# Smaller array tiles in window attention, other slots in two scans, a rewritten last MLP, and x loaded in quarters

## The chip, the cores and the metric

The kernel runs on one core of one Trainium2 chip. A core has five engines with their own instruction streams: TensorE (matrix multiply; the profile shows its matmuls as PE and its weight loads as PEld), VectorE (DVE), ScalarE (ACT), GpSimd (POOL) and SyncE (SP), which here issues all DMAs. They meet through semaphores only. The metric is the device time of one execution in microseconds (us); a lower time is better. All data are float32 unless said otherwise.

## The reference, cut to what matters

Four images of 256 channels and 64x64 pixels go one after the other through four layers. Layers one and two are the same attention block with other weights, layer three is a Mamba block with inner width 512 and 16 states, layer four ("grouped") runs a Mamba of inner width 128 on each of four groups of 64 channels, followed by an MLP. The core of each:

```python
# attention (layers 1 and 2): after a group norm, two gated 1x1 paths and a scan over rows give y
q, k, v = split(to_windows(y) @ qkv_w.T + qkv_b)       # 64 windows of 64 pixels
idx = top_k(mean(q) @ mean(k).T, 4)                     # each window picks 4 windows
attn = softmax((q * C**-0.5) @ k[idx].T)                # 8 heads of 32 channels, 64 queries, 256 keys
out = from_windows(attn @ v[idx]) + depthwise3x3(v)     # "lepe"
x = x + out @ wo.T + wo_b
# Mamba (layers 3 and 4)
u = silu(causal_conv4(in_proj(norm(x))))
dt, B, C = split(x_proj(u));  delta = softplus(dt_proj(dt))
h[t] = exp(delta[t] * A) * h[t-1] + delta[t] * u[t] * B[t]
y[t] = sum_n C[t, n] * h[t, :, n] + D * u[t];   m = y * silu(z) @ out_proj
# layer 4 then, per group
m = gelu(layernorm(m) @ fc1 + b1) @ fc2 + b2 + skip * xn
out = x + silu(batchnorm(outc @ m))
```

## The kernel before

Channels lie on the 128 partitions, in two halves; x of one image (128 x 8192) stays in on-chip memory from its load until the last layer has added its result and stored it. `net_kernel` loops over the four images: it loads x with two DMAs (L1934), then calls `attention_layers`, `mamba_layer` and `grouped_mamba_layer`. The tile pools use a manual schedule: each engine runs its instructions in the order in which the Python code emits them, and waits only where a tile is not ready or a buffer not free.

**Attention.** Each of the two layers has a scan phase over 8 strips of 8 image columns (`scan_phase`), a routing step, and a window phase (`window_phase`) over 32 pairs of windows. One turn `i` of the pair loop emits, in this order: the gathers of pair i+2 (DMA), `scores(i + 1)`, the softmax parts `smallest`, `exps` and `normalise` of pair i+1 interleaved with `turn` and `turned` of pair i (the transposes of the probabilities on TensorE and the copies out of PSUM), one projection of 1x1 kind (`queries` or `project`), and `values(i)`. `own_rows(i - 1)` adds the attention output to the image of the depthwise convolution. GpSimd normalises the probabilities and does 36 of the depthwise taps (`taps`, spread over the first 27 turns). In the first attention layer steps of the next layer's group norm (`gn`) are placed on turns, in the second the statistics of x for the next norm (`stats`); both put instructions on VectorE, ScalarE, GpSimd and TensorE by the dictionaries `mids` and `ends`.

The query tile `qbuf` holds each 64-row block twice, with two heads side by side and zeros where the other head stands, so that one matmul of 64 rows by 128 columns gives the scores of two heads for 64 queries. The zeros are written once per image by 16 memsets (L105). A pair needs 16 score matmuls and 16 value matmuls; in the records each float32 matmul is two passes, each with its weight load. A value matmul takes 128 rows by 64 columns, and yields for two heads also the products of one head's probabilities with the other head's values; `own_rows` takes the rows that belong to each head, in four additions of 32 rows.

**The scans.** `scan_blocks` runs both Mamba layers. A block is 128 inner channels by 1024 pixels, a slot is one of its 16 states. Per slot VectorE multiplies `du` with the broadcast B (`pb`, L914) and scans (L920), GpSimd multiplies with the broadcast C (`hc`, L926), ScalarE computes the decay (L856; `dap` where it lies in PSUM), and TensorE broadcasts B from a table split into bfloat16 parts (`spread`, L844) and sums up y through transposes (`turn`, L872). Three states of a block are treated "apart": their B comes by DMA and GpSimd does the multiplication (L830). All else of the layer, for the next block or the one before, is placed by hand on slots: `put(block, slots, steps)` appends steps to a slot's list `bg`, which the loop emits after that slot's scan. The steps that matter here are `x_proj` (projections, then two copies on ScalarE and two subtractions on GpSimd that split the table: `xs`), `delta` (softplus: a matmul, then Abs, Exp and Ln on ScalarE, then an addition on VectorE, per half; last the product `du` on GpSimd), `silu` (needs another table set on ScalarE, and back), `mlp` (seven steps for each half of 512 pixels), `norm`, `out_conv` and `out`. In the grouped layer a chunk of 1024 pixels has four blocks, two pairs of an `even` and an `odd` block.

**The end of an image.** After the last block of the grouped layer the code emits the rest of the MLP of the pair before (`late`), then the last pair's MLP one half after the other with all table changes, then four output convolutions, their Silu, four additions on GpSimd and the stores. Then the next image's x is loaded.

Of the kernel before, what the change touches and what calls it, by code (L numbers as in the profile page):

```python
# [24 lines left out]
NH = 4  # L25
# [20 lines left out]
class Net:  # L46
# [33 lines left out]
    def attention_layers(self, x, w_drams, v_drams):  # L80
        tc, nc = self.tc, self.nc
        with ExitStack() as ctx:
# [17 lines left out]
                [big.tile([P, 2, NW, 2, 64], F32, name=f"q{i}{m}") for m in range(2)]  # L100
                for i in range(2)
            ]
            for t in qbuf[0] + qbuf[1]:
                for r in range(0, P, 32):
                    nc.gpsimd.memset(t[r : r + 32, :, :, 1 - r // 32 % 2, :], 0.0)  # L105
# [151 lines left out]
            def queries(lay, s, m, psum):  # L257
# [4 lines left out]
                def evict():  # L262
                    for h in range(NH):
                        rows = slice(h * 32, h * 32 + 32)
                        b, h2 = divmod(h, 2)
                        nc.scalar.activation(
                            q[rows, b, :, h2, :].rearrange("p w (j i) -> p w j i", i=8),
                            ps[rows].rearrange("p (j w i) -> p w j i", j=8, i=8),
                            AF.Identity, bias=lay["neg_bq"][rows, m : m + 1], scale=-SCALE,
                        )  # L270
# [163 lines left out]
            def window_phase(lay, work, psum, idx, nxt):  # L434
# [31 lines left out]
                sc = {}  # L466
# [3 lines left out]
                def scores(i):  # L470
                    sj, a = divmod(i, 4)
                    for w in range(2 if i < n_pair else 0):
                        sc[w] = psum.tile([P, 2, 4, P], F32, tag="sc", name="sc", bufs=2)
                        t = kv[i, w]
                        for cq in range(4):
                            m, b = divmod(cq, 2)
                            for r in range(2):
                                rows = slice(r * 64, r * 64 + 64)
                                k0 = b * P + m * 64
                                nc.tensor.matmul(  # L480
                                    sc[w][:, r, cq, :],
                                    qbuf[sj % 2][m][rows, b, 2 * a + w].rearrange("p h t -> p (h t)"),
                                    t[rows, :, k0 : k0 + 64], start=True, stop=True,
                                )

                mn = {}

                def smallest(i, w):
                    if i < n_pair:
                        mn[w] = self.small.tile([P, 4], F32, tag="mn", name="mn", bufs=4)  # L490
                        nc.vector.tensor_reduce(  # L491
                            mn[w], sc[w].rearrange("p r c n -> p c r n"), AX.XY, ALU.min
                        )

                def exps(i, w, part=range(4)):
                    if i < n_pair:
                        if 0 in part:
                            sm[i, w] = self.small.tile([P, 4], F32, tag="sm", name="sm", bufs=4)
                            pr[i, w] = work.tile([P, 4, 2, 2, 64], F32, tag="pr", name="pr", bufs=2)
                        t = pr[i, w]  # L500
                        for cq in part:
                            nc.scalar.activation(  # L502
                                t[:, cq].rearrange("p j r t -> p r j t"),
                                sc[w][:, :, cq, :].rearrange("p r (j t) -> p r j t", j=2),
                                AF.Exp, bias=mn[w][:, cq : cq + 1], scale=-1.0,
                                accum_out=sm[i, w][:, cq : cq + 1],
                            )

                def normalise(i, w):
                    if i < n_pair:  # L510
                        t, s = pr[i, w], sm.pop((i, w))
                        nc.vector.reciprocal(s, s)  # L512
                        t = t.rearrange("p c j r t -> p c (j r t)")
# [7 lines left out]
                def turn(i, w):  # L521
                    pt[w] = [
                        psum.tile([P, 4, P], F32, tag="pt", name="pt_ps", bufs=2) for j in range(2)
                    ]
                    t = pr.pop((i, w))
                    for j in range(2):
                        for cq in range(4):
                            nc.tensor.transpose(  # L528
                                pt[w][j][:, cq, :], t[:, cq, j].rearrange("p r t -> p (r t)"),
                                self.ident,  # L530
                            )
                    pts[w] = [
# [4 lines left out]
                def turned(w, j):  # L537
                    if j == 0:
                        nc.vector.tensor_copy(pts[w][0], pt[w][0])
                    else:  # L540
                        nc.scalar.activation(pts[w][1], pt[w][1], AF.Copy)  # L541

                def values(i, w):
                    if w == 0:
                        ov[i] = psum.tile([P, 2, 2, 8, 2, 8], F32, tag="ov", name="ov_ps", bufs=1)
                    t = kv.pop((i, w))
                    for m in range(2):
                        for j in range(2):
                            for b in range(2):
                                cq = 2 * m + b  # L550
                                c0 = C + cq * 64
                                nc.tensor.matmul(  # L552
                                    ov[i][b * 64 : b * 64 + 64, m, :, :, w, :],
                                    t[:, j, c0 : c0 + 64], pts[w][j][:, cq, :],
                                    start=(j == 0), stop=(j == 1),
                                )


                def own_rows(i):
                    if i >= 0:  # L560
                        sj, a = divmod(i, 4)
                        for r in range(4):
                            rows = slice(r * 32, r * 32 + 32)
                            out = vimg[rows, :, 8 * sj : 8 * sj + 8, 1 + a * 16 : 17 + a * 16]
                            nc.vector.tensor_tensor(  # L565
                                out, ov[i][rows, :, r % 2].rearrange("p m j w i -> p m j (w i)"),
                                out, ALU.add,
                            )
                        del ov[i]
# [20 lines left out]
                for w in range(2):  # L590
                    smallest(0, w)
                    exps(0, w)
                    normalise(0, w)
# [26 lines left out]
                for i in range(n_pair):  # L620
# [35 lines left out]
                    values(i, 0)  # L656
                    values(i, 1)
# [457 lines left out]
    def mamba_layer(self, x, bridge, pe_dram, w_in, w_cw, w_x, w_dt, w_out, v_dram):  # L1115
        tc, nc = self.tc, self.nc
        ND = 4
        with ExitStack() as ctx:
# [228 lines left out]
            for k in range(n_chunk):  # L1347
# [27 lines left out]
                if more:  # L1375
# [25 lines left out]
                    put(3, (7, 8, 8, 9, 9, 10, 11, 12), xs)  # L1401
                    put(3, (9, 10, 10, 11, 12), delta(k + 1, 0))
# [88 lines left out]
    def grouped_mamba_layer(self, x, bridge, begun, ws_dram, outc_dram, v_dram, out_b):  # L1491
        tc, nc = self.tc, self.nc
        w_in, w_cw, w_x, w_dt, w_out, w_f1, w_f2 = ws_dram
        with ExitStack() as ctx:
# [212 lines left out]
            def out_conv(k, s, m):  # L1707
                def step():
# [6 lines left out]
                    if s == 0 and m == 0:  # L1715
                        chunks[k]["yo"] = work.tile([P, 4, NT], F32, tag="hid", name="yo", bufs=1)
                    nc.scalar.activation(
                        yo(k, s, m), ps, AF.Identity, bias=bnb[:, m : m + 1], scale=bns[:, m : m + 1]
# [13 lines left out]
            def out(k, s, m):  # L1732
                def step():
                    t0 = k * NC + s
                    xs = x[:, m * T + t0 : m * T + t0 + NT]
                    nc.gpsimd.tensor_tensor(yo(k, s, m), xs, yo(k, s, m), ALU.add)
# [115 lines left out]
            for i, (k, c) in enumerate(pairs):  # L1852
# [12 lines left out]
                if more:  # L1865
                    h0, h1 = (self.later(lambda k=k, s=s: norm(k + 1, s), 5) for s in range(2))
                    put(even, (0,), (lambda k=k: begin(k + 1),))
                    put(even, (0, 1, 4, 5, 6), h0)
                    put(even, (14, 15), h1)
                    put(odd, (1, 2, 3), h1[2:])  # L1870
                put(even, (4, 5, 6, 7, 8, 9), x_proj(k, 2 * c + 1))
                if i:
                    m0, m1 = mlp(*pairs[i - 1], 0), mlp(*pairs[i - 1], 1)
                    put(even, (5, 6, 7, 10, 11, 12, 13), m0)
                    put(even, (6, 7, 8), m1)
# [3 lines left out]
                    else:  # L1879
# [150 lines left out]
```

## Time and profile before

| | us |
|---|---|
| median of 3 runs (12438.44 to 12444.25) | 12441.65 |
| the profiled execution, its own time | 12439.35 |
| its span, first to last instruction | 12437.6 |
| mean granted TensorE clock (share of full speed) | 0.922 |
| period from image to image (x loads to x loads) | about 3109 |
| window phases of the second image | 3340 to 3625 and 3820 to 4125 |
| scan of the Mamba layer, same image | 4180 to 5150 |
| scan of the grouped layer, same image | 5220 to 6140 |

The profile is one execution, taken by the hardware profiler. In a group's line stand the source line, the engine, the operation, the tile written and those read, the shape, the count, the busy time with the mean duration of one, and the idle time before it with what ended most of it. The chain of waits, followed back from the last instruction, holds only some 18% of the span here, all in the last image, so stages are read one by one instead. Some of the rows that carry the work of the window phase:

```profile
L514 POOL TENSOR_TENSOR pr<-pr,sm 128x1024 f32<-128x1024 f32 x512 | 967.9, 1897 | 560.0 <-DVE sm L512 380.6
L552 PE MATMUL ov_ps<-pts,kv 128*64 128x128 f32 x8192 | 583.6, 289 | 91.6 <-DVE vimg L565 75.6
L480 PE MATMUL sc<-kv,q 64*128 64x128 f32 x8192 | 573.0, 288 | 81.7 <-DMA kv<-kv_dram 68.0
L565 DVE TENSOR_TENSOR vimg<-ov_ps,vimg 32x256 f32<-32x256 f32 x1024 | 428.1, 418 | 12.1 <-PE ov_ps L552 1.6
L266 ACT ACTIVATE q<-conv_ps,neg_bq 32x512 f32<-32x512 f32 x512 | 346.4, 677 | 25.4 <-PE conv_ps L208 19.0
```

In a matmul's row "64*128" is the part of the array it uses, rows by columns. Matmuls overlap, so a mean duration of 289 ns says less than the distance between starts.

### The profile page before, as it was taken

The numbers are of one execution on the slowest core, as the hardware profiler recorded it, in microseconds if no ns is written. First come the engines' busy times: TensorE is split into PE (matmuls) and PEld (weight loads), VectorE is DVE, ScalarE is ACT, GpSimd is POOL, SyncE is SP. The second block draws the span as 40 slices with busy tenths as digits, with TensorE's granted clock in tenths as the row PEclk, the third lists the DMA queues.
The fourth block names the chain that finished last, engine by engine and source line by source line (L and its number), as shares of the span: only waits on it lengthen the run. The fifth ranks groups of instructions, "written<-read, shape, count | busy, mean of one in ns | idle before, by whom it ended". The sixth has DMA issues, their size and how long they took to land. (4 is left out here: it accounts for less than half of the span.)

```text
span 12437.6 us, 159552 instructions
## 1 busy us (share of the span) xinstructions
PE 10255.9 (82%) x54592; PEld 6015.9 (48%) x54592; DVE 10216.3 (82%) x9130; ACT 7245.9 (58%) x13300; POOL 9018.9 (73%) x4634
## 2 busy tenths in 40 slices
PE   8987887787898788777789878877878987887777
PEld 4664544443466454444346645444434664544443
DVE  6777898897677799889767779988976777998897
ACT  4565554776466555477645655547754565554775
POOL 4666886887466688688746668868874666886887
PEclk9999998999899999899889999989988999998998
DMA  3343554454334455454433434545543343554454
GB/s 96 108 128 131 168 169 147 167 169 142 97 108 127 132 169 170 146 168 167 144 95 109 127 130 172 169 146 167 169 142 95 109 127 130 172 170 146 167 170 140
DMA packets 680299, 1773.54 MB, mean 143 GB/s; under 512 B 89120, under 2 KB 195120, under 8 KB 678464
## 3 DMA queue, kind: packets, MB, share of 16 engines
q1 hardware_dynamic: 679488, 1763.34, 43.7%
q8 instruction: 435, 7.13, 0.2%
q14 instruction: 376, 3.08, 0.1%
HBM read 1601.51 MB, written 94.37 MB: 136 GB/s over the span
## 5 line engine op out<-in xcount | busy, mean ns | idle before, releaser
L926 POOL TENSOR_TENSOR hc<-h,cb 128x1024 f32<-128x1024 f32 x2056 | 4814.1, 2350 | 988.2 <-DVE h L920 425.6
L920 DVE TENSOR_TENSOR_SCAN h<-da,m_state,pb 128x1024 f32<-128x1024 f32 x1248 | 2919.9, 2340 | 161.7 <-DVE pb L914 2.8
L872 PE MATMUL y<-ident,hc 128*128 128x128 f32 x16384 | 2371.0, 293 | 346.7 <-POOL hc L926 259.0
L872 PEld LDWEIGHTS y<-ident,hc 128*128 128x128 f32 x16384 | 2091.8, 152 | 1009.7 <-POOL hc L926 439.0
L914 DVE TENSOR_TENSOR pb<-du,pb 128x1024 f32<-128x1024 f32 x1672 | 2024.8, 1211 | 92.5 <-PE pb L844 89.3
L856 ACT ACTIVATE da<-delta,m_v 128x1024 f32<-128x1024 f32 x1672 | 1898.8, 1141 | 220.8 <-DVE h L920 204.0
L844 PE MATMUL pb<-m_parts,pick 128*128 128x512 bf16 x3312 | 1099.8, 417 | 872.2 <-DVE h L920 821.8
L502 ACT ACTIVATE pr<-sc,mn 128x256 f32<-128x256 f32 x2048 | 956.6, 478 | 770.8 <-PE pt_ps L528 551.2
L514 POOL TENSOR_TENSOR pr<-pr,sm 128x1024 f32<-128x1024 f32 x512 | 967.9, 1897 | 560.0 <-DVE sm L512 380.6
L844 PEld LDWEIGHTS <-pick 128*128 128x128 bf16 x3312 | 255.2, 101 | 1883.1 <-DVE h L920 1160.3
L920 DVE TENSOR_TENSOR_SCAN h<-da,pb 128x1024 f32<-128x1024 f32 x424 | 969.6, 2287 | 55.6 <-DVE pb L914 1.4
L830 POOL TENSOR_TENSOR bb<-du,bb 128x1024 f32<-128x1024 f32 x376 | 888.8, 2364 | 65.2 <-DMA bb<-m_cd 60.5
L491 DVE TENSOR_REDUCE mn<-sc 128x4 f32<-128x1024 f32 x512 | 609.6, 1219 | 244.9 <-PE sc L480 242.8
L920 DVE TENSOR_TENSOR_SCAN h<-dap,m_state,bb 128x1024 f32<-128x1024 f32 x288 | 672.0, 2333 | 76.2 <-ACT dap L856 63.4
L528 PE MATMUL pt_ps<-ident,pr 128*128 128x128 f32 x4096 | 571.6, 283 | 145.7 <-ACT pts L541 64.3
L208 PE MATMUL conv_ps<-att_y,att_wb 128*128 128x512 f32 x1536 | 688.8, 593 | 0.0
L856 ACT ACTIVATE dap<-delta,m_v 128x1024 f32<-128x1024 f32 x376 | 419.6, 1116 | 422.3 <-DVE h L920 298.2
L552 PE MATMUL ov_ps<-pts,kv 128*64 128x128 f32 x8192 | 583.6, 289 | 91.6 <-DVE vimg L565 75.6
L480 PE MATMUL sc<-kv,q 64*128 64x128 f32 x8192 | 573.0, 288 | 81.7 <-DMA kv<-kv_dram 68.0
L528 PEld LDWEIGHTS pt_ps<-ident,pr 128*128 128x128 f32 x4096 | 465.8, 144 | 315.4 <-issue 151.4
L480 PEld LDWEIGHTS sc<-kv,q 64*128 64x128 f32 x8192 | 515.8, 196 | 124.3 <-issue 56.1
L552 PEld LDWEIGHTS ov_ps<-pts,kv 128*64 128x64 f32 x8192 | 456.4, 141 | 217.2 <-DVE vimg L565 131.9
(270 smaller groups left out, 18063.0 us busy)
## 6 DMA issues: line engine op xcount, KB each, us to landing
cb<-m_cd SPq DMA_DIRECT2D x2048, 512.0 KB
kv<-kv_dram SPq DMA_DIRECT2D x2048, 128.0 KB
bb<-m_cd SPq DMA_DIRECT2D x376, 512.0 KB
q<-q SPq DMA_DIRECT2D x256, 256.0 KB
kv_dram<-kst SPq DMA_DIRECT2D x128, 256.0 KB
kv_dram<-vn SPq DMA_DIRECT2D x128, 256.0 KB
x<-in_x_dram SPq DMA_DIRECT2D x8, 2048.0 KB
m_pe<-in_pe_dram SPq DMA_DIRECT2D x32, 512.0 KB
```

The lines of the kernel that those rows point to most:

```text
L480: nc.tensor.matmul(sc[w][:, r, cq, :], qbuf[sj % 2][m][rows, b, 2 * a + w].rearrange("p h t -> p (h t)"), t[rows, :, k0 : k0 + 64], start= ...
L502: nc.scalar.activation(t[:, cq].rearrange("p j r t -> p r j t"), sc[w][:, :, cq, :].rearrange("p r (j t) -> p r j t", j=2), AF.Exp, bias=m ...
L514: nc.gpsimd.tensor_tensor(t, t, s.rearrange("p (a o) -> p a o", o=1).to_broadcast([P, 4, 256]), ALU.mult,)
L528: nc.tensor.transpose(pt[w][j][:, cq, :], t[:, cq, j].rearrange("p r t -> p (r t)"), self.ident,)
L552: nc.tensor.matmul(ov[i][b * 64 : b * 64 + 64, m, :, :, w, :], t[:, j, c0 : c0 + 64], pts[w][j][:, cq, :], start=(j == 0), stop=(j == 1),)
L830: nc.gpsimd.tensor_tensor(pb[i], slots[i][0]["du"], pb[i], ALU.mult)
L844: nc.tensor.matmul(pb[i][:, ss], self.pick[:, n : n + 1].to_broadcast([P, P]), blk["parts"][:, ss], start=True, stop=True,)
L856: nc.scalar.activation(da[i], blk["delta"], AF.Exp, scale=blk["a"](n))
L872: nc.tensor.matmul(blk["y"][:, ss], t[:, ss], self.ident, is_transpose=True, start=(n == 0 and ss.start % NT == 0), stop=(n == DS - 1 and ...
L914: nc.vector.tensor_tensor(pb[i], blk["du"], pb[i], ALU.mult)
L920: nc.vector.tensor_tensor_scan(h[i][:, ss], da[i][:, ss], pb[i][:, ss], state, ALU.mult, ALU.add)
L926: nc.gpsimd.tensor_tensor(hc[i][:, ss], h[i][:, ss], cb[i][:, ss], ALU.mult)
```

## The change

Five edits. (1) In window attention `qbuf` loses its zeros and its memsets; a head's 32 rows are one row tile. Scores are computed by 32 matmuls of 32 rows by 64 columns for a pair, the tiles of PSUM and of probabilities hold the heads of one parity (`h`) for both windows, not one window (`w`) for all heads. Values are 32 matmuls of 128 rows by 32 columns with 64 moving columns, `own_rows` is one addition of 128 rows, the query eviction two instructions for four. The tile `pr` gets four buffers for two. (2) In the Mamba layer the steps of `delta` and the splitting steps of `x_proj` in a chunk's fourth block get other slots. (3) In the grouped layer `x_proj`, `delta`, `mlp`, `norm`, `out_conv` and the Silu of u get other slots. (4) The last pair's MLP is written out with both halves of pixels side by side: squares for both, four Gelus of 1024 columns without a table change between them, Silu taken in the output convolution's own eviction, the last additions on VectorE. The MLP of the pair before it moves into slots of the last block. (5) x is one tile for all images; the next image's x is loaded by chunks of 1024 pixels, three of them in slot 8 of a block in the grouped layer, the last one at the image's end.

```diff
-                [big.tile([P, 2, NW, 2, 64], F32, name=f"q{i}{m}") for m in range(2)]
+                [big.tile([P, 2, NW, 64], F32, name=f"q{i}{m}") for m in range(2)]
...
-            for t in qbuf[0] + qbuf[1]:
-                for r in range(0, P, 32):
-                    nc.gpsimd.memset(t[r : r + 32, :, :, 1 - r // 32 % 2, :], 0.0)
...
-                    for h in range(NH):
-                        rows = slice(h * 32, h * 32 + 32)
-                        b, h2 = divmod(h, 2)
+                    for b in range(2):
+                        rows = slice(b * 64, b * 64 + 64)
...
+                        for h in range(2):
+                            sc[h] = psum.tile([P, 2, 2, 2, P], F32, tag="sc", name="sc", bufs=2)
+                        for w in range(2):
+                            for m in range(2):
+                                for r in range(2):
+                                    for h in range(2):
+                                        r0 = r * 64 + h * 32
+                                        rows = slice(r0, r0 + 32)
+                                        for b in range(2):
+                                            k0 = b * P + m * 64
+                                            nc.tensor.matmul(
+                                                sc[h][b * 64 : b * 64 + 64, r, w, m, :],
+                                                qbuf[sj % 2][m][rows, b, 2 * a + w],
+                                                kv[i, w][rows, :, k0 : k0 + 64],
+                                                start=True, stop=True,
+                                            )
...
-                            pr[i, w] = work.tile([P, 4, 2, 2, 64], F32, tag="pr", name="pr", bufs=2)
+                            pr[i, h] = work.tile([P, 4, 2, 2, 64], F32, tag="pr", name="pr", bufs=4)
...
+                def values(i):
+                    ov[i] = psum.tile([P, 2, 8, 2, 8], F32, tag="ov", name="ov_ps", bufs=1)
+                    for w in range(2):
+                        t = kv.pop((i, w))
+                        for m in range(2):
+                            for j in range(2):
+                                for h in range(2):
+                                    for b in range(2):
+                                        p0 = b * 64 + h * 32
+                                        c0 = C + m * P + p0
+                                        nc.tensor.matmul(
+                                            ov[i][p0 : p0 + 32, m, :, w, :],
+                                            t[:, j, c0 : c0 + 32],
+                                            pts[h][j][:, 2 * w + m, b * 64 : b * 64 + 64],
+                                            start=(j == 0), stop=(j == 1),
+                                        )
...
-                        for r in range(4):
-                            rows = slice(r * 32, r * 32 + 32)
-                            out = vimg[rows, :, 8 * sj : 8 * sj + 8, 1 + a * 16 : 17 + a * 16]
+                        out = vimg[:, :, 8 * sj : 8 * sj + 8, 1 + a * 16 : 17 + a * 16]
...
-                    put(3, (7, 8, 8, 9, 9, 10, 11, 12), xs)
-                    put(3, (9, 10, 10, 11, 12), delta(k + 1, 0))
+                    put(3, (7, 8, 8, 9), xs)
+                    put(3, (10, 11, 11, 12, 12), delta(k + 1, 0))
+                    put(3, (10, 11, 12, 13), xs[4:])
...
-                    put(even, (0, 1, 4, 5, 6), h0)
+                    put(even, (0, 1, 13, 14, 15), h0)
...
-                put(even, (4, 5, 6, 7, 8, 9), x_proj(k, 2 * c + 1))
+                xs, ds = x_proj(k, 2 * c + 1), delta(k, 2 * c + 1)
+                put(even, (4, 5), xs)
+                put(even, (8, 9, 9, 10, 10) if c else (7, 8, 8, 9, 9), ds)
+                put(even, (10, 11, 12, 13), xs[2:])
...
-                    put(even, (5, 6, 7, 10, 11, 12, 13), m0)
-                    put(even, (6, 7, 8), m1)
+                    put(even, (10, 11, 12) if c else (9, 10, 11), m1)
+                    put(even, (6, 7, 8, 11, 12, 13, 13) if c else (5, 6, 7, 10, 11, 12, 13), m0)
...
-                    else:
+                    elif i + 1 < len(pairs):
                         put(odd, (15,), m1[3:])
                         late.append(((0, 1, 1), m1[4:]))
-                put(even, (7, 8, 8, 9, 10), delta(k, 2 * c + 1))
+                    else:
+                        put(odd, (3, 4, 5, 6), m1[3:])
...
+                    put(even, (8,), [lambda k=k: load(slice((k - 1) * NC, k * NC))])
...
-                    put(odd, (10, 12, 15), [out_conv(k - 1, *sm) for sm in outs[:3]])
+                    put(odd, (13, 14, 15), [out_conv(k - 1, *sm) for sm in outs[:3]])
...
-                    put(odd, (4, 5, 6, 7), all_u(nk, ncol))
-                    put(odd, (7,), (silu(nk, ncol, "u"),))
-                    put(odd, (8, 8, 8, 9, 10, 11), x_proj(nk, 2 * ncol))
-                    put(odd, (9, 10, 10, 11, 12), delta(nk, 2 * ncol))
+                    put(odd, (3, 4, 5, 6), all_u(nk, ncol))
+                    put(odd, (6,), (silu(nk, ncol, "u"),))
+                    xs = x_proj(nk, 2 * ncol)
+                    put(odd, (8, 9), xs)
+                    put(odd, (10, 11, 11, 12, 12), delta(nk, 2 * ncol))
+                    put(odd, (10, 11, 12, 13), xs[2:])
...
+            for s in range(2):
+                for f in range(2):
+                    ps = psb.tile([P, 2, NT], F32, tag="pb", name="f1_ps")
+                    for g, r in enumerate((lower, upper)):
+                        nc.tensor.matmul(
+                            ps[:, g], wf1[r, f * P : (f + 1) * P], sq[s][r, 1, :],
+                            start=True, stop=True,
+                        )
...
+                    nc.scalar.activation(hid[s, f], ps, AF.Gelu, bias=f1b[:, f : f + 1])
...
+            for s in (0, NT):
+                for m in range(2):
+                    out_conv(k, s, m, AF.Silu)()
+                    out(k, s, m, nc.vector)()
+            load(slice(k * NC, T))
...
+    x = xp.tile([P, 2 * T], F32, name="x")
+
+    def load(b, ts):
+        if b < NB:
+            nc.sync.dma_start(
+                x.rearrange("p (c t) -> p c t", c=2)[:, :, ts], x_dram[b][:, :, ts]
+            )
```

## The prediction

> **What bounds the kernel now.** I read the page's busy shares first. No engine is full over the span, so the answer must come from stages:
>
> ```profile
> span 12437.6 us, 159552 instructions
> PE 10255.9 (82%) x54592; PEld 6015.9 (48%) x54592; DVE 10216.3 (82%) x9130; ACT 7245.9 (58%) x13300; POOL 9018.9 (73%) x4634
> ```
>
> Next the busy time by stage for the second image (3108 to 6217 us), from the view of windows: the two window phases, the third layer's scan and the image's end.
>
> ```profile
> core 0: us, PE busy (x) PEld busy (x) DVE busy (x) ACT busy (x) POOL busy (x), PEclk, DMA share, GB/s
> 3340.00:3625.00 285.00, 255.25 (x2667) 197.87 (x2668) 210.50 (x352) 190.45 (x629) 223.01 (x139) 0.95 0.49 142
> ...
> 3820.00:4125.00 305.00, 263.68 (x2698) 203.21 (x2698) 222.62 (x373) 192.87 (x631) 227.88 (x140) 0.95 0.45 131
> ...
> 5220.00:6140.00 920.00, 713.45 (x3361) 395.27 (x3359) 833.03 (x508) 637.12 (x926) 815.49 (x369) 0.91 0.50 170
> 6140.00:6217.00 77.00, 51.75 (x168) 22.86 (x168) 23.59 (x16) 33.34 (x43) 24.69 (x16) 0.82 0.10 40
> ```
>
> TensorE leads the window phases (255 of 285, with a slow start inside). The third layer is VectorE's (833 of 920), with GpSimd close behind (815). At the image's end nobody is busy: a dependent chain. Then the timeline of one window pair, TensorE first:
>
> ```profile
> 3511.42 2.06 PE L480 MATMUL sc<-kv,q 64*128 64x128 f32 x32
> 3513.41 1.09 PE L528 MATMUL pt_ps<-ident,pr 128*128 128x128 f32 x8
> 3514.34 1.88 PE L208 MATMUL conv_ps<-att_y,att_wb 128*128 128x512 f32 x4
> 3516.05 1.04 PE L528 MATMUL pt_ps<-ident,pr 128*128 128x128 f32 x8
> 3517.27 2.35 PE L552 MATMUL ov_ps<-pts,kv 128*64 128x128 f32 x32 [0.17 <-DVE vimg L565]
> 3519.55 2.06 PE L480 MATMUL sc<-kv,q 64*128 64x128 f32 x32
> ```
>
> One pair takes 8.13 us (3511.42 to 3519.55) and TensorE is idle 0.2 of it: TensorE sets the pace. The others of the same pair wait for it; ScalarE's wait is for a `pr` buffer that the transposes still read:
>
> ```profile
> 3514.59 0.47 ACT L502 ACTIVATE pr<-sc,mn 128x256 f32<-128x256 f32 x1 [3.11 <-PE pt_ps L528]
> 3515.50 1.71 DVE L565 TENSOR_TENSOR vimg<-ov_ps,vimg 32x256 f32<-32x256 f32 x4
> ```
>
> What VectorE waits for in the third layer (total us, times, longest):
>
> ```profile
> DVE delta L1049 <- ACT delta L1045: 33.7, 20, 2.6
> DVE pb L914 <- PE pb L844: 15.1, 12, 4.5
> DVE h L920 <- ACT dap L856: 11.7, 3, 4.2
> ```
>
> And the seam between two images, from the timeline:
>
> ```profile
> 3059.55 1.08 ACT L883 ACTIVATE du<-y 128x512 f32<-128x512 f32 x2 [15.61 <-PE y L872]
> ...
> 3105.58 4.93 POOL L1736 TENSOR_TENSOR yo<-x,yo 128x512 f32<-128x512 f32 x4 [26.45 <-ACT yo L1730]
> ...
> 3110.97 0.87 SPq L1934 DMA_DIRECT2D x<-in_x_dram  x2
> ...
> 3124.61 2.34 DVE L149 TENSOR_REDUCE gn_s<-x 128x4 f32<-128x1024 f32 x2
> ```
>
> From the last scan's output to the first sum of the next image 65 us pass, 14 of them for x.
>
> **What the Trainium skill says.** TensorEngine Tiling (Array Packing), Key Properties: tiles work independently, LdWeights included, and a change of tiling mode drains the array. The trace agrees for two tiles: in the records of L480 both tiles' matmuls start 6 to 7 ns apart, and a step of two takes 111 ns, where one full-array transpose record takes 109; entering the scores costs some 0.1 us. TensorE: Matmul & The Clock Gate, Part 3, reports up to 16 tiles at once (10.6 times); no run here shows over two. The same page, Part 1, gives a floor: matmul starts never closer than about 25 ns, or 62 ns each when the sequencer decodes them in software. The 6 to 7 ns speak against both across tiles, but only for two tiles per 111 ns. Tiling, Gotcha 1: row tiles must not share a PSUM bank; here r and h pick four banks, so nothing serializes there.
>
> **Attention, per pair.** Scores: 16 matmuls (32 records, two passes each) in two tiles are 16 steps of 0.111. They become 32 matmuls (64 records) in eight tiles: 8 steps, 0.9 us for 1.78. Values: 16 in two tiles of 128 columns become 32 in four tiles of 64 columns: 16 steps of about 0.057 (half of 0.109), 0.9 for 1.75. VectorE's four row additions become one: 3 x 0.418 = 1.25 us less. The query eviction is 2 instructions for 4 (677 ns each), 1.35 less on ScalarE in every second pair. `pr` in four buffers ends the 3.11 us wait.
>
> What is late next? TensorE's work falls to about 6.4 us. But score tiles are now split by head parity, both complete only when all 32 matmuls are done, and the next scores wait for the last exponential. That is a closed loop. From the start of scores: 1.25 until VectorE may begin (8 steps, 0.27 last matmul, pickup), 1.22 minimum, 0.06, ScalarE 5.01 (3514.59 to 3519.60: eight exponentials, two copies), 0.05: 7.59 us. GpSimd per pair: 2 x 1.87 normalise and, in the first 27 pairs, 4/3 taps x 2.86: 7.55 us. Values end at about 7.5 too, as their second half waits for the last copy near 6.6. Three limits meet, so I take 7.65 against 8.13: 0.47 x 24 pairs = 11 us for the first layer, plus some 5 in its last five pairs (8.6, 8.5, 7.9, 12.1 and 9.6 apart), where GpSimd has no taps. In the second layer the group statistics make pairs of 11 to 12 us: VectorE's reduce waits for a square queued behind the 2.75 us eviction, and the second minimum waits behind that. The shorter eviction frees it, but GpSimd adds 2.47 for each centring: per pair 7.55 + 5 x 2.47/25 = 8.04, say 8.2 for 25 pairs that now take 219.7: 15 us, and 4 in the rest. Sum 16 + 19 = 35 per image, 140 us. Bounds per image: 55 less (no GpSimd limit) to 20 more (steps with half the tiles).
>
> **Image start.** For three images only the last quarter of x is loaded there. Now 4 MB land 13.3 us after issue; a quarter of the moving time (some 11.3, the rest taken as fixed) gives about 5 us, with the constants behind it 5.8 for 14.1: 8.3 x 3 = 25. The 15.7 us of memsets on GpSimd end at 3126.86, just when the mean is ready; they'd bind if they stayed. Image one gains 1. Bounds 6 to 9 each. The other quarters go through SP at slot 8, after the output stores of slots 4 and 5, whose additions already released that part of x; DMA is half busy there. I cost them at nothing; if a quarter delays the next table broadcasts it is 3 us, nine times: 27.
>
> **Image end.** The previous pair's MLP remainder (gelu, fc2: 3060.64 to 3072) moves into slots 3 to 6 of the last block, where ScalarE has only decays; hidden. The rest, redone with rows of the trace from 3059.55: copies and final transposes to 3063.7, out_proj, squares 3066.3, rsqrt 3068.9, one table load, four gelus of 128x1024 (1.1 each) to 3074.8, fc2 3079.2, xo 3080, table load, four output convolutions of 1.72 from 3079.2 with Silu straight out of PSUM, last addition on VectorE 3087.7. Before: 3110.5. So 22.8 x 4 = 91. Bounds 15 to 26.
>
> **Slots of the scans.** Third layer: delta waits come where its Abs, Exp and Ln queue on ScalarE behind a Silu with two table loads (4.6 us in slot 7) or behind MLP squares and bf16 copies; the 4.2 us of `dap` where Silu, normalisation and MLP meet. Delta moves ahead of the splitting copies (now slots 10 to 13), the Silu one slot earlier, norm's second part to 13 to 15. This takes away 33.7 + 9 = 43. What is new: slots 10 to 15 now hold gelus, copies, rsqrt and out_conv; the split table is ready at 13 and read by TensorE at 15, so `pb` waits (15.1) stay and grow. I net 28 per image, 112; bounds 50 less, 10 more. Second layer: three delta waits of 2.0, 1.9 and 3.1 in the fourth block; 5 per image, 20.
>
> **Sum.** 140 + 26 + 91 + 112 + 20 = 389 off the profiled execution's 12439.35 (span 12437.6 and 1.75 around it), 12050; the median of the runs is 2.3 higher: 12053.
>
> **Rivals.**
> - Half the tiles (four at once for scores, two for values). For: no run shows more than two. Against: the 6 to 7 ns. Each loop is 0.9 longer, 8.5 per pair, so attention loses some 30 in all after the shorter evictions; 12440 - 249 + 30 = 12220.
> - The slot moves only shift stalls: GpSimd is 89% busy in that layer. Without 132: 12185.
> - Slower: TensorE takes each matmul record singly at 62 ns. Place: 128 score and value records a pair. Scores 64 x 0.062 = 4.0, loop 4.4 + 1.22 + 5.1 = 10.7, 2.6 x 240 pairs less 40 = 580 more, against 249 gained elsewhere: 12770. It decides from about 42 ns a record (loop 9.1, which eats the 249). Against it: two tiles already give a record every 55 ns and start 7 ns apart.
> - More than forecast: GpSimd doesn't hold attention, the third layer gives 45 an image: 11890.
>
> **How the numbers follow.** Forecast 0.66, half tiles 0.12, slots for nothing 0.10, more 0.05, slower 0.07. The likeliest one's own range is 11940 to 12160; taking in the half-tile and slot cases 11890 to 12260. About 0.2% (25 us) can be told from no change. Faster 0.91, same 0.02, slower 0.07.
>
> **What would show it.** A pair of scores within 1.3 us, values about 1.2; pairs 7.6 apart; no `pr` wait on pt_ps, instead ScalarE waiting for the minimum; the pairs of 11 us gone; delta waits under 10 us an image; 28 us from du to the last addition, 6 from there to the first sum. Wrong if scores still last 2 us, or if `pb` waits grow by what delta loses.

## The result: 0.4% faster, and the profile after

| | before | after |
|---|---|---|
| median of 6 runs each, us | 12442.95 (12424.85 to 12448.97) | 12393.26 (12378.34 to 12413.69) |
| ratio, 95% interval | | 0.9963 (0.995 to 0.9976) |
| span of the profiled execution, us | 12437.6 | 12385.0 |

The forecast was 12053, so 50 us came for 389. First the page's busy shares of the kernel after:

```profile
span 12385.0 us, 191463 instructions
...
PE 10004.2 (81%) x70976; PEld 5697.7 (46%) x70976; DVE 9900.7 (80%) x8386; ACT 7032.4 (57%) x13000; POOL 8928.3 (72%) x4546
```

All five are less busy than before, in a span only 53 us shorter: work did go, and waits came. Where, is seen by cutting both traces at the same events (first and last score, first and last scan instruction of a layer, first sum of an image), summed over the four images, in us:

| stage | before | after | change | forecast |
|---|---|---|---|---|
| window phases of attention layer 1 | 1084.9 | 1058.2 | -26.8 | -64 |
| window phases of attention layer 2 | 1126.3 | 1055.2 | -71.1 | -76 |
| from there to the Mamba layer's scan | 344.2 | 330.6 | -13.6 | |
| scan of the Mamba layer | 3819.9 | 3792.1 | -27.9 | -20 |
| scan of the grouped layer | 3871.8 | 4076.3 | **+204.6** | **-112** |
| image end and start of the next | 262.3 | 147.9 | -114.4 | -117 |
| the rest | 1914.3 | 1910.6 | -3.7 | |

One stage has the wrong sign, and alone takes back four fifths of what the others gain. The view of windows for the second image (columns: stretch, its length, then the engines' busy times, granted clock and DMA share) has the two window phases, the grouped layer's scan and the image's end:

```profile
core 0: us, PE busy (x) PEld busy (x) DVE busy (x) ACT busy (x) POOL busy (x), PEclk, DMA share, GB/s
3340.00:3610.00 270.00, 227.57 (x4620) 156.65 (x4619) 158.10 (x243) 167.42 (x585) 221.35 (x138) 0.95 0.46 131
3820.00:4080.00 260.00, 218.42 (x4608) 152.07 (x4606) 165.33 (x259) 168.65 (x583) 223.62 (x138) 0.95 0.47 132
5160.00:6160.00 1000.00, 756.64 (x3444) 418.96 (x3440) 856.48 (x521) 659.40 (x952) 837.85 (x380) 0.89 0.50 165
6169.00:6207.00 38.00, 26.78 (x89) 10.38 (x87) 6.08 (x9) 16.97 (x22) 2.60 (x4) 0.90 0.20 68
```

In the grouped layer VectorE's share was 833 of 920 (91%) and is 856 of 1000 (86%): more idle time on the engine that bounds the stage. These stretches are a little shorter than the scan; over the whole of it VectorE is busy 875 us before and 876 after, so its work stayed the same. What it waits for there (total us in that stretch, times, longest):

```profile
DVE pb L912 <- PE pb L842: 52.4, 31, 5.4
DVE h L918 <- ACT dap L854: 45.7, 10, 5.8
DVE delta L1047 <- ACT delta L1043: 7.5, 4, 2.4
DVE h L918 <- POOL bb L828: 7.3, 9, 2.0
```

Against the lines of before: delta 33.7 to 7.5, as forecast; `pb` 15.1 to 52.4; `dap` 11.7 to 45.7; `bb` 1.3 to 7.3. Sum: -26.2 + 37.3 + 34.0 + 6.0 = 51.1 us an image, which is the stage's 51. (Taken over the whole scan, each of these waits is within 0.6 us of the value given.) So two new waits are to be explained.

**The dap wait.** The timeline around one of the seven long ones in an image (start, duration, engine; in brackets idle time and what ended it):

```profile
5366.56 1.26 ACT L1581 ACTIVATE m_u<-u_ps,m_v 128x512 f32<-128x512 f32 x2 [4.18 <-PE u_ps L1574]
5367.84 1.28 ACT L1606 ACT_TABLE_LOAD   x1
...
5369.14 2.00 ACT L1606 ACTIVATE m_u<-m_u 128x1024 f32<-128x1024 f32 x2
...
5371.16 1.28 ACT L948 ACT_TABLE_LOAD   x1
...
5372.45 1.12 ACT L854 ACTIVATE dap<-delta,m_v 128x1024 f32<-128x1024 f32 x1
...
5373.67 2.29 DVE L918 TENSOR_TENSOR_SCAN h<-dap,bb 128x1024 f32<-128x1024 f32 x1 [5.82 <-ACT dap L854]
```

`scan_blocks` issues the decay of a state that is treated apart (states 0, 4 and 8) two slots ahead, as the last thing of the slot, behind its background steps. The change puts the Silu of the odd blocks from slot 7 into slot 6, and the decay of state 8 is issued at the end of slot 6: it stands behind 4.6 us of table load, Silu and table load (5367.84 to 5372.45). The scan has waited since 5367.85, so it pays all of that and the decay itself, 1.1 us. In slot 7 nothing of the sort follows.

**The pb wait.** The timeline of a third block's slots 11 to 14:

```profile
5318.57 2.14 POOL L1082 TENSOR_TENSOR m_bct<-m_bct,m_parts 64x1024 f32<-64x1024 f32 x1
...
5320.75 1.06 ACT L1079 ACTIVATE m_parts<-m_bct 64x1024 bf16<-64x1024 f32 x1 [3.86 <-POOL m_bct L1082]
5321.82 1.28 ACT L1670 ACT_TABLE_LOAD   x1
...
5323.11 1.27 ACT L1670 ACTIVATE hid<-f_ps,m_f1b 128x512 f32<-128x512 f32 x2
...
5323.85 2.65 PE L1663 MATMUL f_ps<-m_sq,m_wf 64*128 64x512 f32 x4 [6.33 <-ACT hid L1670]
...
5326.44 1.04 PE L842 MATMUL pb<-m_parts,pick 128*128 128x512 bf16 x2
...
5327.51 1.23 DVE L912 TENSOR_TENSOR pb<-du,pb 128x1024 f32<-128x1024 f32 x1 [4.82 <-PE pb L842]
```

Read it upwards from the last line: VectorE waits for the spread of B, which is queued on TensorE behind the second hidden product of the MLP (L1663), which waits for the Gelu to free its PSUM, which is queued on ScalarE behind the second splitting copy, which waits 3.86 us for GpSimd's remainder. The splitting steps were in slots 6 to 9 before, away from the Gelu.

**The pair of windows** (TensorE, SyncE and ScalarE, in the phase that the prediction's profile shows, one pair earlier):

```profile
3473.26 6.13 SPq L456 DMA_DIRECT2D kv<-kv_dram  x8
...
3474.77 0.47 ACT L501 ACTIVATE pr<-sc,mn 128x256 f32<-128x256 f32 x1 [2.01 <-DVE mn L490]
...
3477.41 0.30 PE L555 MATMUL ov_ps<-pts,kv 128*32 128x64 f32 x4
...
3478.14 0.32 PE L555 MATMUL ov_ps<-pts,kv 128*32 128x64 f32 x8 [0.41 <-DVE pts L540]
...
3478.64 0.98 PE L555 MATMUL ov_ps<-pts,kv 128*32 128x64 f32 x52 [0.19 <-ACT pts L542]
...
3479.55 0.78 PE L480 MATMUL sc<-kv,q 32*64 32x128 f32 x32
...
3480.71 1.41 PE L480 MATMUL sc<-kv,q 32*64 32x128 f32 x32 [0.38 <-DMA kv<-kv_dram]
```

ScalarE no longer waits for `pr` but for the minimum, as forecast. New is the break inside the scores: the second window's keys are late. The pair's eight loads take 6.1 us to issue, and a load lands 2.6 us after its issue (median); together that is 8.7 us, more than the 7.4 us that the fastest pairs now take. A load must wait until the values of an earlier pair have freed a `kv` buffer, and SyncE can't make up for such a wait: between 3400 and 3560 us it stands idle for 9.6 us, and otherwise it issues loads, stores of the queries and reads of the window numbers with no gap over 0.12 us. The loads shown come late in such an unbroken run, which began at 3463.84 after a wait of 1.6 us. The pair distance in the first layer, steady at 8.1 in the middle of the phase before, is now 7.4 to 8.9 there, median 8.0.

**The seam between images:**

```profile
3069.30 1.09 ACT L881 ACTIVATE du<-y 128x512 f32<-128x512 f32 x2 [16.09 <-PE y L870]
...
3097.09 0.69 DVE L1736 TENSOR_TENSOR yo<-x,yo 128x512 f32<-128x512 f32 x1 [1.03 <-ACT yo L1717]
...
3098.24 0.39 SPq L1974 DMA_DIRECT2D x<-in_x_dram  x1
...
3104.68 2.34 DVE L145 TENSOR_REDUCE gn_s<-x 128x4 f32<-128x1024 f32 x2
```

From the last `du` to the last addition 28.5 us (forecast 28), from there to the first sum 6.9 (forecast 6), 35 for 65.

### The profile page after: what moved, and what is told of

The parts are those of the page before. It is cut to its first block, busy times and chain, and to the rows that moved or that the text cites. A ratio compares the mean times of both kernels' runs of the same rounds, so it can differ in the third digit from the quotient of the medians.

```text
span 12385.0 us, 191463 instructions
## 1 busy us (share of the span) xinstructions
PE 10004.2 (81%) x70976; PEld 5697.7 (46%) x70976; DVE 9900.7 (80%) x8386; ACT 7032.4 (57%) x13000; POOL 8928.3 (72%) x4546
## 5 line engine op out<-in xcount | busy, mean ns | idle before, releaser
L480 PE MATMUL sc<-kv,q 32*64 32x128 f32 x16384 | 408.9, 300 | 151.5 <-DMA kv<-kv_dram 96.7
L555 PE MATMUL ov_ps<-pts,kv 128*32 128x64 f32 x16384 | 432.8, 234 | 113.7 <-DVE pts L540 66.1
L240 DVE SCALAR_TENSOR_TENSOR lp<-vimg,att_v,lp 128x512 f32<-128x512 f32 x616 | 465.5, 756 | 27.9 <-DVE lp L240 0.5
L204 PE MATMUL conv_ps<-att_xn,att_wa 128*128 128x512 f32 x1024 | 462.1, 605 | 14.2 <-POOL att_xn L180 14.2
```

The source lines that it names most:

```text
L204: nc.tensor.matmul(ps, w[:, k, w0 + m * P : w0 + (m + 1) * P], src[:, k], start=(k == 0), stop=(k == 1),)
```

## The experiments

Every run is compared with the kernel before on the same chip, 4 runs of each variant, whose medians stand below (before: 12431 to 12443); what lies between two variants is read from their ratios to before and from the stages. First all of them (grouped: scan of that layer, mean of the four images; windows: both layers, four images summed):

| kernel | us | ratio to before, 95% interval | grouped, us | windows, us |
|---|---|---|---|---|
| before | 12443 | 1 | 968 | 2211 |
| after | 12393 | 0.9963 (0.995 to 0.9976) | 1019 | 2113 |
| e1, Silu in slot 7 | 12222 | 0.9826 (0.981 to 0.9843) | 976 | 2117 |
| e2, splitting early | 12296 | 0.9889 (0.9872 to 0.9905) | 998 | 2111 |
| e4, all slots as before | 12182 | 0.9795 (0.9778 to 0.9811) | 967 | 2114 |
| e5, eight kv buffers | 12352 | 0.9931 (0.9914 to 0.9948) | 1019 | 2079 |
| e6, decay ahead of the steps | 12298 | 0.9883 (0.9867 to 0.99) | 989 | 2116 |
| e7, before with Silu in slot 6 | 12552 | 1.0088 (1.0072 to 1.0105) | 996 | 2223 |
| e8, three repairs | 12095 | 0.9724 (0.9707 to 0.974) | 952 | 2085 |
| e9, four repairs | 12070 | 0.9702 (0.9686 to 0.9718) | 948 | 2078 |
| e10, e9 with two pr buffers | 12214 | 0.9818 (0.9802 to 0.9835) | 946 | 2212 |
| e11, e9 with the MLP early | 12105 | 0.9727 (0.9711 to 0.9743) | 955 | 2083 |

### Is it the slots at all? (e4)

All `put` calls of the grouped layer as before, but for the loads of x and the MLP that the new tail needs in the last block.

> The kernel after, with all slots of the grouped layer as in the kernel before (odd and even blocks, output convolutions); attention, image end, image start and the second layer stay as in after. If the slots alone cost what the stage table shows, the scan of that layer falls from 1019 to 967 us an image and the time to 12393 - 205 = 12188. If it is the loads of x or the new tail around it that disturb the scan, it stays near 1019 and 12393.

12182: the scan is back at 967 us. The slots cost the 205 us; the loads of x in slot 8 and the new tail cost this scan nothing.

### The Silu of u (e1, e6, e7)

```diff
-                    put(odd, (3, 4, 5, 6), all_u(nk, ncol))
-                    put(odd, (6,), (silu(nk, ncol, "u"),))
+                    put(odd, (4, 5, 6, 7), all_u(nk, ncol))
+                    put(odd, (7,), (silu(nk, ncol, "u"),))
```

> The kernel after, with one edit in the grouped layer: the four u steps of the odd blocks in slots 4 to 7 and their Silu in slot 7, as in the kernel before (after has 3 to 6 and 6). Theory A (the Silu with its two table loads, 4.6 us, now sits in slot 6, ahead of the decay for slot 8, which is issued at the end of slot 6 and goes to the scan through PSUM): the dap waits of 5.6 to 5.8 us, seven in an image, go; 7 x 5.7 = 40 us an image, 160 in all, about 12235. Rival B (the delta steps, not the Silu, are what the slot paid for: with the Silu back in slot 7 the delta waits of 2.3 us come back on every odd block): 7 x 4 = 28 us an image are given back, 12345. Rival C (the loss lies with the splitting copies of the even blocks): no change, 12393.

12222, the scan 171 us shorter in all. VectorE's waits in the same image of e1:

```profile
DVE pb L912 <- PE pb L842: 27.6, 12, 4.8
DVE pb L912 <- PE f_ps L1691: 12.7, 4, 4.7
DVE pb L912 <- PE f_ps L1663: 10.4, 9, 2.2
DVE delta L1047 <- ACT delta L1043: 7.8, 5, 2.4
...
DVE h L918 <- ACT dap L854: 6.5, 4, 2.4
```

`dap` falls from 45.7 to 6.5, delta stays at 7.8: the gain on delta never needed the earlier Silu, and rival B falls. The `pb` waits, 50.7 in three lines, are untouched. Next, is it the place in the queue, or only that ScalarE is crowded there? In e6 the Silu stays in slot 6 and the decay is issued ahead of the steps:

```diff
+            decay(i + 2, True)
             for step in blk["bg"].get(n, ()):
                 step()
...
             turn(i - 1)
-            decay(i + 2, True)
```

> The kernel after, slots untouched (the odd Silu stays in slot 6), but in every scan the decay that goes through PSUM is issued ahead of the slot's background steps, not behind them. If the place in ScalarE's queue is the cause (theory A), this gives what the Silu in slot 7 gave: the dap waits go, about 170 us in the grouped layer, 12225. If it is the crowding of ScalarE around slots 6 to 8 whatever the order (rival), the same work is still there and the scan stays near 1019 us an image, 12390.

The grouped scan is 119 us shorter in all, not 171, and the Mamba layer's, where the order changes too, 28 us longer than in after: 12298. No `dap` line is left among the waits, but a smaller one has come (a stretch of the same image):

```profile
DVE pb L912 <- PE pb L842: 53.6, 31, 5.5
...
DVE h L918 <- ACT m_state L859: 15.1, 6, 2.7
```

`m_state` is the copy of the last column of a scan's result, which ScalarE makes a slot later and which now stands behind the Silu in its turn. So the place in the queue decides, and every decay or copy behind the Silu counts, not `dap` alone. Last, the converse, the kernel before with the two lines of e1 reversed:

> The kernel BEFORE with one edit: u steps of the odd blocks in slots 3 to 6 and their Silu in slot 6. Theory A: seven dap waits of some 5.7 us an image come in (160 us in all), while the delta steps behind, two slots away from the Silu now, lose part of their 33 us an image (half of them lie in odd blocks, at most 16 x 4 = 64): slower by 95 to 160, 12530 to 12600. Rival (an earlier Silu only relieves the delta steps; the loss of after comes from other moves together with it): faster by up to 60, 12380.

12552, 0.9% slower than before: the grouped scan is 28 us an image longer. Its waits:

```profile
DVE h L920 <- ACT dap L856: 52.5, 11, 6.0
DVE delta L1049 <- ACT delta L1045: 21.2, 15, 2.4
```

Before they were 11.7 and 33.7. The move alone makes this loss: it gives 12 us of delta for 41 of `dap`.

### The splitting copies (e2)

```diff
-                put(even, (10, 11, 12, 13), xs[2:])
+                put(even, (6, 7, 8, 9), xs[2:])
```

> The kernel after, with one edit in the grouped layer: the splitting steps of the even blocks (bf16 parts of B and C) in slots 6 to 9, as in the kernel before, not 10 to 13. Theory A2 (in slots 12 to 14 of the third block of a chunk ScalarE's second copy waits for GpSimd's remainder, the Gelu is queued behind that copy, the second hidden product on TensorE behind the Gelu, and the spread for VectorE's next slot behind that product): the pb waits of 4.7 and 3.5 us go, (3 x 8.2 + 4.7) = 29 us an image, less some delta waits that come back (4 x 2.3 an image); net 20 an image, 80 in all, 12313. Rival (the pb waits come from the second part of the normalisation, moved to slots 13 to 15, or from TensorE's load there): the waits stay, 12393, or 12430 if delta waits return.

12296, the grouped scan 85 us shorter. Waits of VectorE in e2:

```profile
DVE h L918 <- ACT dap L854: 48.0, 11, 6.0
DVE pb L912 <- PE pb L842: 15.1, 15, 4.6
DVE pb L912 <- PE f_ps L1663: 9.0, 6, 2.2
DVE delta L1047 <- ACT delta L1043: 8.4, 6, 2.3
...
DVE pb L912 <- PE f_ps L1691: 6.1, 2, 3.2
```

`pb` is 30.2 in three lines for 52.4, `dap` as in after, and delta doesn't come back, though the splitting of the even blocks is ahead of it again. So for the delta waits this move wasn't needed either. In the odd blocks the splitting copies stay in slots 10 to 13 in all runs but e4 and e7; what they do there wasn't tried alone.

### The loads of keys and values (e5)

```diff
-    kv[i, w] = t = work.tile([P, 2, 2 * C], F32, tag="kv", name="kv", bufs=6)
+    kv[i, w] = t = work.tile([P, 2, 2 * C], F32, tag="kv", name="kv", bufs=8)
```

> The kernel after, with eight buffers for the gathered keys and values instead of six. Theory K (gather is a closed loop: a pair's eight loads start only when the values of the pair before have read their buffers, take 6.1 us to issue on SP and 2.6 to land, 8.7 us, while the scores want them 7.4 us later): the waits of the scores for kv go and pairs come down to about 7.6; 240 pairs x 0.3 = 70 us, about 12320; at the least the 5.1 and 3.4 us that TensorE is seen waiting, 34 in all, 12360. Rival G (GpSimd's 7.55 us a pair sets the pace, the loads are late only because nothing pulls them): pairs stay at 8.0, 12380 to 12393.

12352. TensorE's row for the scores in the first layer's window phase, first of after, then of e5:

```profile
L480 PE MATMUL sc<-kv,q 32*64 32x128 f32 x1920 | 47.5, 294 | 5.3 <-DMA kv<-kv_dram 5.1
```

```profile
L480 PE MATMUL sc<-kv,q 32*64 32x128 f32 x1920 | 41.3, 286 | 0.7 <-issue 0.7
```

No wait for a load is left, SyncE stands idle 1.8 us of 160 (3390 to 3550) for 9.6, and the pairs of the first layer have a median of 7.48 us for 7.99 (same image). That layer gains 33 us over four images, nearly all of its half of the 70 us expected for both; the second gains only 1.5, and there two pairs with group statistics take 11.5 and 11.0 us. Theory K holds for the first layer; what holds the second wasn't separated.

At the new pace GpSimd is close behind: over 18 pairs in the middle of the first layer (3372 to 3508 us) a pair takes 7.55 us on average and GpSimd is busy 94% (88% in after, at 8.0 us a pair). Every third pair takes 7.9 us and most others 7.4, and every third turn has two depthwise taps where the others have one. So GpSimd didn't cause the 8.0 us of after, which rival G said, but it and SyncE leave next to no room below 7.5.

### Together, and what is left (e8 to e11)

> The kernel after with three repairs: Silu of the odd blocks in slot 7, splitting of the even blocks in slots 6 to 9, eight buffers for keys and values. If the three causes are independent the gains add: 12393 - 171 - 97 - 41 = 12084. If they overlap (a wait that one removes is taken by another), less: 12130 or more.

12095: the three gains add up to within 11 us. e9 puts the normalisation back as well:

```diff
-                    put(even, (0, 1, 13, 14, 15), h0)
+                    put(even, (0, 1, 4, 5, 6), h0)
```

> The three repairs and a fourth: the second part of the first normalisation of the third block back in slots 4 to 6 (after has 13 to 15). Theory N (in slots 13 to 15 its matrix products stand on TensorE between the Gelu's products and the spread): pb waits on f_ps of 3 to 5 us go, three an image: 40 us less than the kernel with three repairs, about 12045. Rival (in slots 4 to 6 it meets the Silu of slot 3, which gave the 4.2 us dap waits of before, three an image): 50 more, about 12135.

12070, 25 us less where 40 were expected: the fastest kernel of this study. What VectorE waits for in its grouped layer:

```profile
DVE pb L912 <- PE pb L842: 16.5, 14, 4.4
DVE h L918 <- ACT dap L854: 10.0, 5, 2.4
DVE h L918 <- POOL bb L828: 9.8, 7, 3.2
DVE delta L1047 <- ACT delta L1043: 7.0, 3, 2.4
```

`pb` and `dap` are at the level of before, delta at that of after: the layer is 20 us an image faster than before. Against e8, `pb` falls from 21.9 to 16.5 and `dap` rises from 6.5 to 10.0: the direction of theory N, with a part of what the rival named. Then the buffers of the probabilities:

> The kernel with four repairs (12070), but with two pr buffers instead of four, as in the kernel before. If the closed loop from scores to exponentials sets the pair (theory of the prediction), the second half's exponentials wait some 0.9 us for the transposes of the pair before, and the pair, 7.4 to 7.5 now, becomes 8.3: 240 x 0.9 = 215 us slower, 12285. If another limit (GpSimd, the loads) sets the pace, or the smaller tiles alone made the gain, the wait is absorbed: 12070 to 12120.

12214, 144 us slower: the commonest pair of the first layer takes 7.85 us for 7.38. ScalarE waits for the transposes again: in a steady pair the second half's exponentials start at 3412.22 us after 0.34 us of idle time, just as the transposes that read their buffer have ended (3412.12). (The view puts only the longer waits of this kind down to the transposes.) The mechanism was expected; 0.9 us a pair was about twice too much. The windows come to 2212 us, what they took before the change: with two buffers the smaller tiles and all else in attention bring nothing in sum. Four buffers with the old tiles weren't tried, so what the buffers alone would give isn't known. Last, e11 moves the MLP steps of the even blocks back:

```diff
-                    put(even, (10, 11, 12) if c else (9, 10, 11), m1)
-                    put(even, (6, 7, 8, 11, 12, 13, 13) if c else (5, 6, 7, 10, 11, 12, 13), m0)
+                    put(even, (5, 6, 7, 10, 11, 12, 13), m0)
+                    put(even, (6, 7, 8), m1)
```

> The kernel with four repairs, and the MLP steps of the even blocks back in the slots of before (second half in 6 to 8, first in 5 to 7 and 10 to 13). If the late second half is what still delays the spread on TensorE (pb waits of 16.5 us an image, longest 4.4), they fall by half: 35 us faster, 12035. If it now meets the delta steps, which moved to slots 7 to 10, the delta waits come back by 15 us an image: 12130.

12105, 35 us slower, for neither reason: delta waits are 6.2, so they don't come back, and `pb` waits rise to 20.0 instead of falling; a `dap` wait of 4.3 us is back (`dap` 16.4 in all). The later MLP slots were a good move of the change.

## Why the prediction failed

**The step that failed** is "Slots of the scans", for what the prediction calls the third layer (the grouped layer): "I net 28 per image, 112; bounds 50 less, 10 more." The scan became 51 us an image longer. Three terms of it:

- "Delta moves ahead ...": the 33.7 us did go, to 7.5, and e9 shows that the layer can keep it: 20 us an image better than before, where 28 was forecast. But the size held without the reasons given. With the odd Silu back in slot 7 and the even blocks' splitting copies back in slots 6 to 9, both at once (e8), delta waits are 8.3; with the normalisation back too (e9) 7.0, and with the MLP back too (e11) 6.2. What is left of the change in e11 are the new slots of the delta steps themselves, of the odd blocks' `x_proj` and of the output convolutions; which of them does it wasn't tried.
- "The Silu one slot earlier" stood among the gains, with "33.7 + 9" taken away, the 9 being `dap` waits. What the move puts behind the Silu was priced at nothing. The instruction emitted next on ScalarE is the decay for state 8, and its reader, the scan, is already waiting. So the cost is the Silu with its tables (4.6 us, known from the trace of before) and the decay itself (1.1): 5.7 us, seven times, 40 an image. e1, e6 and e7 show it from three sides. Of the 9 little stays in the end: the waits of 4.2 us are gone in e9, but `dap` is 10.0 in all, for 11.7.
- "`pb` waits (15.1) stay and grow" had the direction; the size, 37 us more, wasn't foreseen. The chain was in sight ("the split table is ready at 13 and read by TensorE at 15"), but the prediction looked at when the table is ready, not at who waits behind the copy: the Gelu, a hidden product, the spread. e2, with the splitting copies back, takes 22 of the 37 away. With the Silu back as well (e8) `pb` is 21.9, and with the normalisation (e9) 16.5.

The prediction's own mark for being wrong, "if `pb` waits grow by what delta loses", came true: 37 against 26.

**Attention**, 140 forecast, 98 found. The sizes of the matrix products held. Scores in eight tiles take 1.26 us, 1.25 was forecast. Values were forecast at 57 ns for a step of four tiles, and where they run without a wait, in the last 52 of a pair's 64 records, a step takes 56. "Values about 1.2" isn't met all the same: the first twelve records wait for copies of the probabilities, and in the pair shown the values take 2.2 us. The closed loop was put at 7.59 us, and the fastest pairs take 7.4. GpSimd's 7.55, an average over turns with one tap and with two, is what the steady pairs of the first layer come to in e5. What was left out is the gather: at 8.1 us a pair it was just hidden, below that it is not. With eight buffers the two window phases stand 132 us under before, near the forecast. Of the pairs over 11 us in the second layer (four in the second image, past the first two pairs) none is over 10.8 now, but with eight buffers two are over 11 again. So the shorter eviction did not free them; what holds them stays open.

**The rest** held: image end and start -114 for -117, the Mamba layer -28 for -20, the loads of x free of charge, the MLP remainder hidden in the last block. The 13.6 us between attention and the Mamba layer were not forecast, and weren't looked into.

Of the rivals, "the slot moves only shift stalls" came nearest, but it stopped at zero. A slot move that makes its stage slower was not among them; the bounds of that term let it cost 10 us an image at most. In the "slower" rival one sum doesn't close: at 42 ns a record its own formula (64 x 0.042 + 0.4 + 1.22 + 5.1) gives a loop of 9.4 us, not 9.1. Nothing else rests on it.

## What to carry to other kernels

When a step with a table change moves on an in-order engine, list what the loop emits after it in the same slot, and ask who reads that next: here the price of a step was set by what stood behind it, not by its own reader. Follow a wait through the queues (copy, Gelu, matmul, broadcast) until it reaches the bounding engine, before calling it hidden. And when a loop is to become faster, price every feed of it at the new pace, issue time and landing included; here the loads were one buffer pair short, and the engine that issues them had no time to catch up.

## What the runs showed of the hardware

- Eight tiles of 32 x 64 work at once in float32: where no key is late, the 64 matmul records of a pair's scores start within 0.99 us, 15.7 ns apart on average and often 6 to 7 ns, and take 1.26 us in all. The floor of about 25 ns from start to start that the Trainium skill gives in TensorE: Matmul & The Clock Gate, Part 1, doesn't show across tiles.
- In four tiles of 128 x 32 with 64 moving columns, 52 records in a row start within 0.76 us, 56 ns for a step of four. Before, a step of two tiles of 128 x 64 with 128 moving columns took 109 ns. The weight load of one of the small tiles has a median of 110 ns, so with four of them in 56 ns the loads of several tiles overlap.
- The Silu begins 1.30 us after its table load begins (5369.14 and 5367.84), and the load begins as soon as the activation before it ends (5367.82). The Trainium skill, ScalarE: Activation LUTs, "What ACT_TABLE_LOAD costs", gives 1.28 us for the load, which agrees, and about 1.38 more for a drain, which this trace doesn't show.
